# An attention block on one core: queries and keys projected three slots ahead, norm weights folded into the rotation tables, the rms factor applied by ScalarE

## The chip, the cores and the metric

The kernel runs on 1 core of one Trainium2 chip. The metric is device time in microseconds (us) of that core, lower is better; the median of three runs is given. One further execution was recorded by the profiler.

## The reference, cut to what matters

Four batches of 1024 tokens with 512 features are normalised (layernorm, no weights), go through an attention with 16 heads of 128, and are added to an fp8-rounded product of the same normalised tokens with a 512x512 matrix.

```python
xn = layernorm(x)
q  = apply_rope(rmsnorm((xn @ Wq + bq).heads, qn_w), pos)       # 16 heads of 128
lk = apply_rope(rmsnorm((xn @ Wlk + blk).heads, kn_w), pos)
lv = (xn @ Wlv + blv).heads
# entries: softmax-weighted mean of every 4 tokens; ck, cv their key and value, one for all heads
ck = apply_rope(rmsnorm(entries @ Wk + bk, kn_w), block_ends);  cv = entries @ Wv + bv
sparse = softmax over the 8 largest of (q . ck, causal), times cv
local  = softmax over a band of 128 tokens back of (q . lk), times lv
out = x + ((sparse + local) * 0.5) @ Wo + bo + fp8(xn * s) @ fp8(W2 * s1) / (s * s1)
# rmsnorm(x, w) = x * rsqrt(mean(x*x) + eps) * w
# rope on the first 64 of 128: x1*cos - x2*sin, x1*sin + x2*cos; the rest unchanged
```

## The kernel before, in words

The tokens are cut into 32 chunks of 128: chunk `t` is chunk `c = t % 8` of its batch. The 16 heads are taken two at a time, which gives 8 units for a chunk, `u = 0..7`, and 256 units in all, n = 8t + u. Everything is written out by hand in one loop over slots (L789): slot s works on several units at once, at different stages, and each engine takes its instructions in the order in which the loop body issues them. In slot s, with t and u of s:

- `scores` (L561): TensorE makes the scores of unit s for both heads in two PSUM banks (`sc`), against the keys of the chunk before (L570), its own (L577) and the compressed entries (L580, 32(c+1) columns).
- `weigh` and `settle` (L590, L621): VectorE masks the window, finds the 8 largest (L603 to L609), ScalarE takes the exponentials (L610, L618), VectorE keeps and scales the chosen ones (L625 to L636), and ScalarE scales the window (L641).
- `queries` (L438): TensorE projects queries and keys of unit s+2 into one bank `qp` (L443), with a bias product (L444). `squares` (L450): ScalarE squares and sums (L294), and `spread` has GpSimd make the factor r = (mean + eps)^-0.5 (L288, L289).
- `turn` (L652) transposes the probabilities of unit s in 32x32 blocks on VectorE, and sends them through DRAM so that they come back turned (`fetch`, L696, SyncE's queue).
- `values_of` (L530): TensorE projects the values of unit s+1 into `vp`; `keep_values` (L544) has ScalarE copy them out. `values` (L706) multiplies the probabilities of unit s-1 with the values into `cp`, `keep_context` (L727) copies that to `cT` on ScalarE, and `to_output` (L744) multiplies unit s-2 with Wo.
- `normalize` (L459) makes rotated and normed queries and keys of unit s+2: four VectorE operations (L465) multiply `qp` by r and the norm weight into `th`; `rotate` (L296) has GpSimd make th*sin into `rb` (L307), VectorE th*cos (L308), a difference and a sum (L309, L310). `turn_keys` and `fetch_keys` (L504, L524) transpose blocks on VectorE (L510, L513), write them to DRAM with four DMAs (L518), and read them back as `qT` and `lkT` (L528). The first eight units and the last instead go through TensorE (`turn_keys_here`, L482, `keep_keys`, L490).

Two generators run beside it, one step at each of the two calls of `steps()` in a slot (L809, L815). `chunk_prep(t+2)` starts in slot u=7 of chunk t and takes nine slots: layernorm statistics on VectorE (L327, L328), the normalised and transposed tokens `xnT`, the entries, and in its last slot (u=7 of chunk t+1) a transpose on TensorE into a bank `cp` of the pool `pp` (L410) that VectorE copies to `ckT` (L412). One slot earlier (u=6) it norms and rotates the entry's key: VectorE L402, then GpSimd `rb_e` (L307). `chunk_eight(t)` starts in slot u=3 of chunk t: three VectorE operations (L261 to L265) and four GpSimd operations (L266, L268, L270, L272) round the tokens to fp8 over two slots; two slots after the start TensorE multiplies them (`fp`, L423), VectorE reads that (L428), and GpSimd adds it to `x_sum` (L429).

PSUM has eight banks: two `qp`, two `sc`, one `ctx`, one `out`, and two of the pool `pp`, which are taken in turn by everything else: `xp`, `yp`, `ep`, the `cp` of `chunk_prep`, `fp`, and every unit's `vp`. A tile of `pp` waits until what stood two tiles before in that order has been read.

The lines of the loop that set the order around the change:

```python
for_unit(s, (weigh, 0), (weigh, 1))
for_unit(s + 2, (queries,))
for_unit(s, (settle, 0), (settle, 1))
steps()
for_unit(s + 2, (squares, (0, 1, 2, 3)), (spread,))
for_unit(s, (settle_window, 0), (settle_window, 1))
for_unit(s - 2, (to_output,))
steps()
turn(s)
for_unit(s + 1, (values_of,))
for_unit(s + 2, (normalize,))
```

Of the kernel before, what the change touches and what calls it, by code (L numbers as in the profile page):

```python
# [12 lines left out]
F32 = mybir.dt.float32  # L13
# [3 lines left out]
ALU = mybir.AluOpType  # L17
AX = mybir.AxisListType

P = 128  # L20
D = 128
RATIO = 4
ROPE = 64
HALF = ROPE // 2
BLK = 32
NB = P // BLK
# [12 lines left out]
def kernel(  # L39
# [26 lines left out]
    nc = tc.nc  # L66
# [4 lines left out]
    NU = NH // 2  # L71
    NE = P // RATIO
    NT = B * NCH
    NN = NT * NU
# [3 lines left out]
    work = ctx.enter_context(tc.tile_pool(name="work", bufs=2))  # L78
# [5 lines left out]
        return v.rearrange("p (b i) -> p b i", i=BLK)  # L84

    def scratch(name, shape=(P, 512), dtype=F32):
        return work.tile(list(shape), dtype, tag="scratch", name=name, bufs=3)

    def pp(name):
        return psum.tile([P, 512], F32, tag="pp", name=name, bufs=2)  # L90
# [5 lines left out]
    x_tiles, angles = {}, {}  # L96

    def load_x(t, purpose):

        b, c = divmod(t, NCH)  # L100
        xt = work.tile([P, HID], F32, tag="x", name=f"x_{purpose}_{t}")
        nc.sync.dma_start(xt, hidden[b, ts(c, P), :])
        x_tiles[purpose, t] = xt
# [15 lines left out]
    wo_sb = [const.tile([P, 2, HID], F32, name=f"wo_{u}") for u in range(NU)]  # L119

    def load_wqk(u, engine):
        for i, w in enumerate((Wq, Wlk)):
            engine.dma_start(
                wqk_sb[u][:, :, ts(i, 256)], w[:, ts(u, 256)].rearrange("(k p) n -> p k n", p=P)
            )
# [34 lines left out]
    norm_w = const.tile([P, 2, D], F32, name="norm_w")  # L160
# [6 lines left out]
    scales = const.tile([P, 2], F32, name="scales")  # L167
# [84 lines left out]
        nc.tensor.transpose(bp[:, 0:NH], blv_n, ident[:NH, :NH])  # L252
        nc.scalar.activation(blvT, bp[:, 0:NH], AF.Copy, scale=0.5)

    def quantize(dst, src, scalar, tag):

        v = scratch(f"qv_{tag}") if tag[0] == "x" else src
        m = scratch(f"qm_{tag}")  # L260
        nc.vector.tensor_scalar(v, src, scalar, None, ALU.mult)  # L261
        nc.vector.tensor_scalar(
            m.bitcast(U32), v.bitcast(U32), 0x7F800000, None, ALU.bitwise_and
        )
        nc.vector.tensor_scalar(m, m, FP8_MIN_NORMAL, 1.5 * 2.0**20, ALU.max, ALU.mult)  # L265
        nc.gpsimd.tensor_tensor(v, v, m, ALU.add)  # L266
        yield
        nc.gpsimd.tensor_tensor(v, v, m, ALU.subtract)  # L268
        yield
        nc.gpsimd.tensor_scalar(m, v, FP8_OVERFLOW, 0.0, ALU.mult, ALU.mult)  # L270
        yield
        nc.gpsimd.tensor_tensor(dst, v, m, ALU.add)  # L272
        yield

    w2_sb = const.tile([P, KK, HID], BF16, name="w2_sb")


    w2_raw = [wo_sb[NU // 2 + k][:, 0, :] for k in range(KK)]

    def round_w2():  # L280
        for k in range(KK):
            yield from quantize(w2_sb[:, k, :], w2_raw[k], scales[:, 1:2], f"w2_{k}")

    def rstd_of(ss, n, mul, eps, name):

# [10 lines left out]
    def rotate(th, cs, nh, a, name):  # L296

        p = th.shape[0]
        a = a.rearrange("p (h t f) -> p h t f", h=nh, t=2)
        bb = work.tile([P, 4, 2, HALF], F32, tag="ropeb", name=f"rb_{name}", bufs=1)  # L300
        bb = bb[:p, 0:nh]
        x12 = th[:, :, 0:ROPE].rearrange("p h (t f) -> p h t f", t=2)

        def wide(v):
            return v.unsqueeze(1).unsqueeze(1).to_broadcast([p, nh, 2, HALF])

        nc.gpsimd.tensor_tensor(bb, x12, wide(cs[:, HALF:ROPE]), ALU.mult)  # L307
        nc.vector.tensor_tensor(a, x12, wide(cs[:, 0:HALF]), ALU.mult)  # L308
        nc.vector.tensor_tensor(x12[:, :, 0, :], a[:, :, 0, :], bb[:, :, 1, :], ALU.subtract)  # L309
        nc.vector.tensor_tensor(x12[:, :, 1, :], a[:, :, 1, :], bb[:, :, 0, :], ALU.add)  # L310
# [104 lines left out]
    def chunk_eight(t):  # L415

        xt, xnT = x_tiles["sum", t], chunks[t]
        x8 = work.tile([P, KK * P], BF16, tag="x8", name=f"x8_{t}", bufs=1)
        src = xnT.rearrange("p k s -> p (k s)")
        yield from quantize(x8, src, scales[:, 0:1], f"x_{t}")  # L420
        fp = pp(f"fp_{t}")
        for k in range(KK):
            nc.tensor.matmul(  # L423
                fp, x8[:, ts(k, P)], w2_sb[:, k, :], start=(k == 0), stop=(k == KK - 1)
            )
        yield
        f = scratch(f"f_{t}")
        nc.vector.scalar_tensor_tensor(f, fp, inv, bo_sb, ALU.mult, ALU.add)  # L428
        nc.gpsimd.tensor_tensor(xt, xt, f, ALU.add)  # L429
# [4 lines left out]
    def place(n):  # L434

        return divmod(n, NU)
# [18 lines left out]
    def spread(n):  # L455
        w = units[n]
        w["r"] = rstd_of(w["ss"], 4, 1.0 / D, EPS_RMS, f"r_{n}")

    def normalize(n):  # L459
        t, u = place(n)  # L460
        w = units[n]
        qp, r = w.pop("qp"), w["r"]
        th = work.tile([P, 4, D], F32, tag="th", name=f"th_{n}", bufs=1)
        for i in range(4):
            nc.vector.scalar_tensor_tensor(  # L465
                th[:, i, :],
                qp[:, ts(i, D)],
                r[:, i : i + 1],
                norm_w[:, i // 2, :],
                ALU.mult,  # L470
                ALU.mult,
            )
        thb = work.tile([P, NB, 2, 2 * BLK], F32, tag="thb", name=f"thb_{n}", bufs=1)
        spare = thb.rearrange("p b t x -> p (b t x)")[:, 0 : 4 * ROPE]
        rotate(th, angles[t][0], 4, spare, f"{n}")
        w["th"], w["thb"] = th, thb

    def by_dma(n):

        return NU <= n < NN - 1  # L480
# [15 lines left out]

    def key_tiles(n):
        w = units[n]
        qT = work.tile([P, NB, 2 * BLK], F32, tag="qT", name=f"qT_{n}")
        lkT = work.tile([P, NB, 2 * BLK], F32, tag="lkT", name=f"lkT_{n}", bufs=NU + 2)  # L500
        w["qT"], w["lkT"] = qT.rearrange("p a (i g) -> p (a i) g", g=2), lkT
        return qT, lkT

# [267 lines left out]
    def until(g, step):  # L771
        for at in g:
            if at == step:
                break

    def for_unit(n, *todo):
        if 0 <= n < NN:
            for f, *more in todo:
                f(n, *more)

    first, rounding = chunk_prep(0), round_w2()
# [4 lines left out]
    pick_tokens()  # L786
    masks()

    for s in range(-2, NN + 2):  # L789
        t, u = place(s)  # L790

        if s == -2 or u == 7 and 0 <= t and t + 2 < NT:
            running = [*running[-2:], chunk_prep(t + 2)]
        if u == 3 and 0 <= t < NT:
            load_x(t, "sum")
            running = [*running[-2:], chunk_eight(t)]
        if u == 4 and 0 <= t and t + 2 < NT:
            load_x(t + 2, "norm")

        for_unit(s, (scores, 0), (scores, 1))  # L800
        for_unit(s - 2, (keep_context,))
        for_unit(s, (weigh, 0), (weigh, 1))
        for_unit(s + 2, (queries,))
        if not by_dma(s + 1) and s < NU:
            for_unit(s + 1, (turn_keys_here,))
        for_unit(s, (settle, 0), (settle, 1))
        if s < 0:
            until(first, "B4" if s == -2 else "B6")
        steps()  # L809
        for_unit(s + 2, (squares, (0, 1, 2, 3)), (spread,))  # L810
        if not by_dma(s + 1) and s < NU:
            for_unit(s + 1, (keep_keys,))
        for_unit(s, (settle_window, 0), (settle_window, 1))
        for_unit(s - 2, (to_output,))
        steps()  # L815
        if by_dma(s):
            turn(s)
        if s == -1:
            until(first, "B7")
        for_unit(s + 1, (values_of,))  # L820
        if s == -1:
            until(first, "B8")
        if not by_dma(s):
            for_unit(s, (turn_here,))
        for_unit(s + 2, (normalize,))
        for_unit(s - 1, (values,))
        if by_dma(s):
            fetch(s)
        else:
            for_unit(s, (keep_turned,))  # L830
        if s + 2 >= NU:
            for_unit(s + 2, (turn_keys,), (fetch_keys,))
        for_unit(s + 1, (keep_values,))
        if s < NU:

            if s == -1:
                late_constants()
                for k in range(KK):
                    nc.scalar.dma_start(w2_raw[k], input2[ts(k, P), :])
            if 0 <= s < KK:  # L840
                for _ in range(4):
                    next(rounding, None)
            if 3 <= s + 5 < NU:
                load_wqk(s + 5, nc.scalar)
            if 3 <= s + 4 < NU:
                load_wlv(s + 4, nc.scalar)
            if 0 <= s + 1 < NU:
                load_wo(s + 1, nc.scalar)
        if u == 6 and 0 <= t and t + 2 < NT:
            load_angles(t + 2)  # L850
        units.pop(s - 1 - NU, None)
# [46 lines left out]
```

## Time and profile before

| what | us |
|---|---|
| median of three runs | 2830.24 (2829.55 to 2833.36) |
| the profiled execution, its own time | 2828.88 |
| its span, first to last instruction | 2827.2 |
| TensorE busy | 2775.0 (98%) |
| VectorE busy | 2277.4 (81%) |
| ScalarE busy | 1302.9 (46%) |
| GpSimd busy | 818.0 (29%) |

All times below count from the span's start. In a timeline a row holds the start, the duration, the engine, the line, the operation, out<-in, shapes and how many instructions were merged in the row; in brackets stand the engine's idle time before it and what ended it. A matmul of two fp32 operands is recorded as two instructions. The ends of matmuls are modelled, and overlap the next start, so that the pace of TensorE is read from start to start. A few matmul records are missing, most of L444 among them (58 of 256 are there).

### The profile page before, as it was taken

Reading aid. Unit: us, or ns where it says so; the run is one execution under the profiler, and the core shown is the slowest. Engines: PE = TensorE matmul, PEld = TensorE weight load, DVE = VectorE, ACT = ScalarE, POOL = GpSimd, SP = SyncE. Lnnn points to the kernel's source line nnn. Section 1 sums busy time; section 2 is a strip of 40 time slices with the busy share of each in tenths; the row PEclk is TensorE's granted clock in tenths of the full one; section 3 lists DMA queues with packets and bytes.
Section 4 is the critical chain, followed back from the end, with each engine's and each line's share of the span. In section 5 each row is a group of like instructions: output and inputs, shape, how many; then the busy total and the mean of one; then the engine's idle time right before and its main releaser. Section 6 shows DMA issues by size and latency. Waiting matters only on the chain. (4 is left out here: it accounts for less than half of the span.)

```text
span 2827.2 us, 48528 instructions
## 1 busy us (share of the span) xinstructions
PE 2775.0 (98%) x12770; PEld 1879.6 (66%) x12969; DVE 2277.4 (81%) x9132; ACT 1302.9 (46%) x5075; POOL 818.0 (29%) x1161
## 2 busy tenths in 40 slices
PE   7999999999999999999999999999999999999998
PEld 4666666666666666666666666666666666666666
DVE  5778888888777888888877788888887777888886
ACT  3444444444444444444444444444444444444443
POOL 3433222222233332232223233222223222322222
PEclk9999999999999999999999999999999999999999
DMA  7344445555444445555544444555554444455553
GB/s 224 93 140 133 137 143 151 147 153 146 133 128 133 138 134 149 148 152 151 148 129 123 137 134 138 150 153 147 149 146 124 134 131 131 136 152 151 149 149 116
DMA packets 620851, 399.85 MB, mean 141 GB/s; under 512 B 306880, under 2 KB 573984, under 8 KB 620576
## 3 DMA queue, kind: packets, MB, share of 16 engines
q1 hardware_dynamic: 608352, 383.18, 47.8%
q10 hardware_dynamic: 12224, 13.56, 1.5%
q8 instruction: 105, 1.72, 0.3%
q14 instruction: 170, 1.39, 0.2%
HBM read 212.53 MB, written 184.03 MB: 140 GB/s over the span
## 5 line engine op out<-in xcount | busy, mean ns | idle before, releaser
L443 PE MATMUL qp<-wqk,xnT 128*128 128x512 f32 x2048 | 944.6, 604 | 4.1 <-DMA scales<-in_L_ffn_scale_dram 3.1
L443 PEld LDWEIGHTS qp<-wqk,xnT 128*128 128x128 f32 x2048 | 370.1, 191 | 383.9 <-issue 370.3
L610 ACT ACTIVATE prob<-sc,neg 128x256 f32<-128x256 f32 (+1 forms) x512 | 236.1, 461 | 786.4 <-DVE taken L609 772.5
L535 PEld LDWEIGHTS vp<-wlv,xnT 128*128 128x128 f32 x2048 | 391.1, 191 | 170.4 <-issue 109.5
L535 PE MATMUL vp<-wlv,xnT 128*128 128x256 f32 x2048 | 488.6, 382 | 6.2 <-DVE lkT L495 2.9
L751 PE MATMUL op<-wo,cT 128*128 128x512 f32 x1024 | 488.0, 599 | 6.0 <-ACT cT L733 1.5
L659 DVE STREAM_TRANSPOSE probB<-prob 128x512 f32<-128x512 f32 (+2 forms) x494 | 282.9, 610 | 79.4 <-ACT prob L641 75.8
L294 ACT ACTIVATE junk<-qp 128x128 bf16<-128x128 f32 x1024 | 284.2, 278 | 100.0 <-remote 56.6
L307 POOL TENSOR_TENSOR rb<-th,cs 128x256 f32<-128x256 f32 x256 | 247.4, 966 | 276.5 <-DVE th L465 276.5
L465 DVE SCALAR_TENSOR_TENSOR th<-qp,r,norm_w 128x128 f32<-128x128 f32 x1024 | 282.9, 338 | 45.1 <-POOL r L289 44.9
L751 PEld LDWEIGHTS op<-wo,cT 128*128 128x128 f32 x1024 | 186.5, 190 | 179.2 <-issue 115.9
L547 ACT COPY lv<-vp 128x256 f32<-128x256 f32 x256 | 95.4, 373 | 449.5 <-PE cp L718 393.5
L288 POOL TENSOR_SCALAR r<-ss 128x4 f32<-128x4 f32 x256 | 49.8, 195 | 862.8 <-ACT junk L294 856.4
L718 PE MATMUL cp<-probT,lv 128*128 128x128 f32 x1920 | 298.3, 275 | 0.7 <-DMA probT<-pr 0.7
L718 PEld LDWEIGHTS cp<-probT,lv 128*128 128x128 f32 x1920 | 275.3, 192 | 14.3 <-PE vp L535 1.1
L289 POOL TENSOR_TENSOR r<-r,nhalf 128x4 f32<-128x4 f32 x256 | 259.9, 1015 | 21.4
L718 PE MATMUL cp<-probT,cv 128*128 128x128 f32 x1536 | 255.6, 275 | 0.0
L580 PE MATMUL sc<-ckT,qT 128*128 128x96 f32 (+7 forms) x1024 | 226.2, 303 | 0.0
L641 ACT ACTIVATE prob<-prob,tot 128x256 f32<-128x256 f32 (+1 forms) x512 | 223.0, 484 | 2.1 <-DVE tot L635 2.0
L309 DVE TENSOR_TENSOR th<-thb,rb 128x128 f32<-128x128 f32 x256 | 87.1, 340 | 158.9 <-POOL rb L307 158.9
L577 PE MATMUL sc<-lkT,qT 128*128 128x128 f32 x1024 | 209.7, 287 | 5.4 <-DMA lkT<-qk 3.9
L718 PEld LDWEIGHTS cp<-probT,cv 128*128 128x128 f32 x1536 | 213.2, 192 | 0.0
(123 smaller groups left out, 4003.8 us busy)
## 6 DMA issues: line engine op xcount, KB each, us to landing
pr<-probB SPq DMA_DIRECT2D x127, 512.0 KB, 2.6
probT<-pr SPq DMA_DIRECT2D x508, 128.0 KB, 2.9
qk<-thb SPq DMA_DIRECT2D x992, 64.0 KB, 2.0
pr<-probB SPq DMA_DIRECT2D x96, 384.0 KB, 2.3
probT<-pr SPq DMA_DIRECT2D x384, 96.0 KB, 2.5
qT<-qk SPq DMA_DIRECT2D x248, 128.0 KB, 2.3
lkT<-qk SPq DMA_DIRECT2D x248, 128.0 KB, 2.5
x_norm<-_attn_hidden_states_dram SPq DMA_DIRECT2D x32, 256.0 KB, 3.1
```

The source lines that it names most:

```text
L289: nc.gpsimd.tensor_tensor(r, r, nhalf[: ss.shape[0], 0:n], ALU.pow)
L294: nc.scalar.activation(junk[: src.shape[0]], src, AF.Square, accum_out=acc)
L307: nc.gpsimd.tensor_tensor(bb, x12, wide(cs[:, HALF:ROPE]), ALU.mult)
L443: nc.tensor.matmul(qp, xnT[:, k, :], wqk_sb[u][:, k, :], start=(k == 0), stop=False)
L465: nc.vector.scalar_tensor_tensor(th[:, i, :], qp[:, ts(i, D)], r[:, i : i + 1], norm_w[:, i // 2, :], ALU.mult, ALU.mult,)
L535: nc.tensor.matmul(vp[:, 0:256], xnT[:, k, :], wlv_sb[u][:, k, :], start=(k == 0), stop=(k == KK - 1),)
L580: nc.tensor.matmul(sc[:, spa], q, ckT[:, 0:m], start=True, stop=False)
L610: nc.scalar.activation(prob[:, loc], sc[:, loc], AF.Exp, bias=neg[:, 0:1], scale=-1.0, accum_out=tot[:, 0:1],)
L641: nc.scalar.mul(prob[:, loc], prob[:, loc], tot[:, 0:1])
L659: nc.vector.transpose(pb[:, :, ds(h * g, g), :], prob[:, parts[0] * P : (parts[-1] + 1) * P].rearrange("p (g b i) -> p b g i", b=NB, i=BLK),)
L718: nc.tensor.matmul(blocks(cp[:, h, :]), v, probT[:, :, h * len(parts) + i - parts[0], :], start=(i == parts[0]), stop=(i == parts[-1]),)
L751: nc.tensor.matmul(op, cT[:, h, :], wo_sb[u][:, h, :], start=(u == 0 and h == 0), stop=(u == NU - 1 and h == 1),)
```

## The change

1. Queries and keys are projected, normed and turned three slots ahead (unit s+3) where it was two, and the loop begins at s = -3. `qT` gets three buffers (it had two), `lkT` NU+3. The weights `wqk` are loaded one slot earlier on ScalarE's queue.
2. `make_tables(t)`, new, runs once for each chunk on GpSimd, in slot u=5 of the chunk before: cosine and sine are multiplied by the norm weights of query and key, the rest of `cos` holds the weights themselves.
3. `normalize`: ScalarE multiplies `qp` by r into `thb` (four operations); GpSimd multiplies the halves, crossed, with `sin` (two operations of 128x128); VectorE multiplies all 512 columns by `cos`, and adds the 256 rotated ones.
4. The shared scratch tiles go from three buffers to two, `chunk_eight(t)` starts in slot u=5 where it was u=3, and the rounding of W2 uses an unused part of the `wo` tiles as its scratch.

```diff
     def scratch(name, shape=(P, 512), dtype=F32):
-        return work.tile(list(shape), dtype, tag="scratch", name=name, bufs=3)
+        return work.tile(list(shape), dtype, tag="scratch", name=name, bufs=2)
...
+    def make_tables(t):
+        cs, _ = angles[t]
...
+        nc.gpsimd.tensor_tensor(
+            cos[:, :, 0:ROPE].rearrange("p g (t f) -> p g t f", t=2),
+            halves, wide(cs[:, 0:HALF], 2, 2), ALU.mult)
+        nc.gpsimd.tensor_copy(cos[:, :, ROPE:D], norm_w[:, :, ROPE:D])
+        nc.gpsimd.tensor_tensor(
+            sin[:, :, 1, :], halves[:, :, 0, :], wide(cs[:, HALF:ROPE], 2), ALU.mult)
+        nc.gpsimd.tensor_scalar(cs[:, HALF:ROPE], cs[:, HALF:ROPE], -1.0, None, ALU.mult)
+        nc.gpsimd.tensor_tensor(
+            sin[:, :, 0, :], halves[:, :, 1, :], wide(cs[:, HALF:ROPE], 2), ALU.mult)
...
     def normalize(n):
...
         for i in range(4):
-            nc.vector.scalar_tensor_tensor(
-                th[:, i, :], qp[:, ts(i, D)], r[:, i : i + 1], norm_w[:, i // 2, :],
-                ALU.mult, ALU.mult)
-        rotate(th, angles[t][0], 4, spare, f"{n}")
+            nc.scalar.mul(xr[:, ts(i, D)], qp[:, ts(i, D)], r[:, i : i + 1])
+        for i in range(2):
+            nc.gpsimd.tensor_tensor(
+                rb[:, :, :, i, :], xr[:, :, :, ds((1 - i) * HALF, HALF)],
+                heads_of(sin[:, :, i, :]), ALU.mult)
+        nc.vector.tensor_tensor(all_, xr, heads_of(cos), ALU.mult)
+        nc.vector.tensor_tensor(
+            turned, turned, rb.rearrange("p g h t f -> p (g h) (t f)"), ALU.add)
...
-    for s in range(-2, NN + 2):
+    for s in range(-3, NN + 2):
...
         if u == 3 and 0 <= t < NT:
             load_x(t, "sum")
+        if u == 5 and 0 <= t < NT:
             running = [*running[-2:], chunk_eight(t)]
...
+        if u == 5 and t + 1 < NT:
+            make_tables(t + 1)
...
-        for_unit(s + 2, (queries,))
+        for_unit(s + 3, (queries,))
...
-        for_unit(s + 2, (squares, (0, 1, 2, 3)), (spread,))
+        for_unit(s + 3, (squares, (0, 1, 2, 3)), (spread,))
...
-        for_unit(s + 2, (normalize,))
+        for_unit(s + 3, (normalize,))
...
-        if s + 2 >= NU:
-            for_unit(s + 2, (turn_keys,), (fetch_keys,))
+        if s + 3 >= NU:
+            for_unit(s + 3, (turn_keys,), (fetch_keys,))
...
-            if 3 <= s + 5 < NU:
-                load_wqk(s + 5, nc.scalar)
+            if 3 <= s + 6 < NU:
+                load_wqk(s + 6, nc.scalar)
```

Line numbers below L458 differ between the two kernels: in the changed one `normalize` stands around L490 to L520, the GpSimd product is L508, the entry's copy to `ckT` L414, and the values' product L579.

More of the change, by code (lines that the diff above doesn't have):

```diff
@@ L253, in late_constants, with quantize @@
         nc.scalar.activation(blvT, bp[:, 0:NH], AF.Copy, scale=0.5)
-    def quantize(dst, src, scalar, tag):
+    def quantize(dst, src, scalar, tag, m=None):
         v = scratch(f"qv_{tag}") if tag[0] == "x" else src
-        m = scratch(f"qm_{tag}")
+        if m is None:
+            m = scratch(f"qm_{tag}")
         nc.vector.tensor_scalar(v, src, scalar, None, ALU.mult)
@@ L281, in round_w2 @@
         for k in range(KK):
-            yield from quantize(w2_sb[:, k, :], w2_raw[k], scales[:, 1:2], f"w2_{k}")
+            spare = wo_sb[NU // 2 + k][:, 1, :]
+            yield from quantize(w2_sb[:, k, :], w2_raw[k], scales[:, 1:2], f"w2_{k}", spare)
     def rstd_of(ss, n, mul, eps, name):
@@ L457, in spread, with wide @@
         w["r"] = rstd_of(w["ss"], 4, 1.0 / D, EPS_RMS, f"r_{n}")
+    tables = {}
+    def make_tables(t):
+        cs, _ = angles[t]
+        cos = work.tile([P, 2, D], F32, tag="cos", name=f"cos_{t}", bufs=1)
+        sin = work.tile([P, 2, 2, HALF], F32, tag="sin", name=f"sin_{t}", bufs=1)
+        halves = norm_w[:, :, 0:ROPE].rearrange("p g (t f) -> p g t f", t=2)
+        def wide(v, *ones):
+            for _ in ones:
+                v = v.unsqueeze(1)
+            return v.to_broadcast([P, *ones, HALF])
+        nc.gpsimd.tensor_tensor(
+            cos[:, :, 0:ROPE].rearrange("p g (t f) -> p g t f", t=2),
+            halves,
+            wide(cs[:, 0:HALF], 2, 2),
+            ALU.mult,
+        )
+        nc.gpsimd.tensor_copy(cos[:, :, ROPE:D], norm_w[:, :, ROPE:D])
+        nc.gpsimd.tensor_tensor(
+            sin[:, :, 1, :], halves[:, :, 0, :], wide(cs[:, HALF:ROPE], 2), ALU.mult
+        )
+        nc.gpsimd.tensor_scalar(cs[:, HALF:ROPE], cs[:, HALF:ROPE], -1.0, None, ALU.mult)
+        nc.gpsimd.tensor_tensor(
+            sin[:, :, 0, :], halves[:, :, 1, :], wide(cs[:, HALF:ROPE], 2), ALU.mult
+        )
+        tables[t] = cos, sin
     def normalize(n):
@@ L462, in normalize, with heads_of @@
         qp, r = w.pop("qp"), w["r"]
+        cos, sin = tables[t]
         th = work.tile([P, 4, D], F32, tag="th", name=f"th_{n}", bufs=1)
+        thb = work.tile([P, NB, 2, 2 * BLK], F32, tag="thb", name=f"thb_{n}", bufs=1)
+        xr = thb.rearrange("p b t x -> p (b t x)")
         for i in range(4):
-            nc.vector.scalar_tensor_tensor(
[L466 to L470, printed above, removed]
+            nc.scalar.mul(xr[:, ts(i, D)], qp[:, ts(i, D)], r[:, i : i + 1])
+        xr = xr.rearrange("p (g h d) -> p g h d", g=2, h=2)
+        rb = work.tile([P, 2, 2, 2, HALF], F32, tag="ropeb", name=f"rb_{n}", bufs=1)
+        def heads_of(v):
+            return v.unsqueeze(2).to_broadcast([P, 2, 2, v.shape[-1]])
+        for i in range(2):
+            nc.gpsimd.tensor_tensor(
+                rb[:, :, :, i, :],
+                xr[:, :, :, ds((1 - i) * HALF, HALF)],
+                heads_of(sin[:, :, i, :]),
                 ALU.mult,
             )
-        thb = work.tile([P, NB, 2, 2 * BLK], F32, tag="thb", name=f"thb_{n}", bufs=1)
-        spare = thb.rearrange("p b t x -> p (b t x)")[:, 0 : 4 * ROPE]
-        rotate(th, angles[t][0], 4, spare, f"{n}")
+        all_ = th.rearrange("p (g h) d -> p g h d", g=2)
+        nc.vector.tensor_tensor(all_, xr, heads_of(cos), ALU.mult)
+        turned = th[:, :, 0:ROPE]
+        nc.vector.tensor_tensor(
+            turned, turned, rb.rearrange("p g h t f -> p (g h) (t f)"), ALU.add
+        )
         w["th"], w["thb"] = th, thb
@@ L498, in key_tiles @@
         w = units[n]
-        qT = work.tile([P, NB, 2 * BLK], F32, tag="qT", name=f"qT_{n}")
-        lkT = work.tile([P, NB, 2 * BLK], F32, tag="lkT", name=f"lkT_{n}", bufs=NU + 2)
+        qT = work.tile([P, NB, 2 * BLK], F32, tag="qT", name=f"qT_{n}", bufs=3)
+        lkT = work.tile([P, NB, 2 * BLK], F32, tag="lkT", name=f"lkT_{n}", bufs=NU + 3)
         w["qT"], w["lkT"] = qT.rearrange("p a (i g) -> p (a i) g", g=2), lkT
@@ L802 @@
         for_unit(s, (weigh, 0), (weigh, 1))
-        for_unit(s + 2, (queries,))
-        if not by_dma(s + 1) and s < NU:
-            for_unit(s + 1, (turn_keys_here,))
+        for_unit(s + 3, (queries,))
+        if s + 2 < NU:
+            for_unit(s + 2, (turn_keys_here,))
         for_unit(s, (settle, 0), (settle, 1))
         if s < 0:
-            until(first, "B4" if s == -2 else "B6")
+            until(first, ("B3", "B4", "B6")[s + 3])
         steps()
-        for_unit(s + 2, (squares, (0, 1, 2, 3)), (spread,))
-        if not by_dma(s + 1) and s < NU:
-            for_unit(s + 1, (keep_keys,))
+        for_unit(s + 3, (squares, (0, 1, 2, 3)), (spread,))
+        if s + 2 < NU:
+            for_unit(s + 2, (keep_keys,))
         for_unit(s, (settle_window, 0), (settle_window, 1))
```

## The prediction

> **What bounds the kernel now.** I read the busy shares first, then TensorE's timeline from start to start, then what ended its gaps, then the queues of GpSimd and VectorE in the slots where the change puts work.
>
> ```profile
> span 2827.2 us, 48528 instructions
> ...
> PE 2775.0 (98%) x12770; PEld 1879.6 (66%) x12969; DVE 2277.4 (81%) x9132; ACT 1302.9 (46%) x5075; POOL 818.0 (29%) x1161
> ```
>
> TensorE's 98% could hide gaps, since matmul ends are modelled. Start to start it is as full as it looks: a projection (L443, eight records) takes 3.44 us, 0.43 each, and in most slots the length is the same to 0.01 us in all four batches (10.01 in chunk 2, u=3; 10.81 in chunk 6, u=6). Such slots have no slack to win, whatever VectorE, ScalarE or GpSimd do in them. What can be won are the slots that are longer than their like. In the timeline of TensorE near 1480 us:
>
> ```profile
> 1478.64 0.39 PE L718 MATMUL cp<-probT,cv 128*128 128x128 f32 x2
> 1480.24 0.47 PE L577 MATMUL sc<-lkT,qT 128*128 128x128 f32 x2 [1.21 <-DMA lkT<-qk]
> ```
>
> From one start to the next 1.60 us pass where 0.22 are usual: the scores wait for keys on their way through DRAM. Adding this excess over all such places (contexts to scores 5.1 and 5.0, first to second score product 3.2) gives 13.4 us in 30 places. That is all that an earlier projection can win in the steady part. The page's waits of TensorE for qT and lkT show less, as they count from modelled ends.
>
> The other waits are at the start. In chunk 0:
>
> ```profile
> 73.09 1.98 PE L751 MATMUL op<-wo,cT 128*128 128x512 f32 x4
> 77.47 3.66 PE L535 MATMUL vp<-wlv,xnT 128*128 128x256 f32 x8 [2.40 <-DVE total L384]
> ```
>
> The values' product waits 2.56 us for a `pp` bank, and its eight matmuls then take 0.43 each instead of 0.215, so another 1.7 us.
>
> **What the Trainium skill says.** "PSUM — Partial Sum Buffer", Engine vs sequencer instructions: ScalarE, VectorE and GpSimd queues are strict FIFO, and matmuls start in program order. The trace agrees; VectorE's rows never leave the loop's order. "Perfetto Trace Analysis", Optimization Strategy: a gap that repeats on the engine that should be saturated can mean too few PSUM buffers; the gap at 75 us is one. "SBUF — State Buffer", SBUF: two separate sides: a VectorE operation with two SBUF inputs and a GpSimd operation exclude each other for a whole instruction. The trace agrees: L309 takes 0.29 us, and 0.69 beside GpSimd's L270 (below). "TensorE: Matmul & The Clock Gate", What's actually happening: an idle window of about 3.4 us halves the clock. Here waits of 2.26 and 2.56 us did it, 1.57 didn't.
>
> **The change part by part.**
>
> *One slot more for keys.* All 13.4 us go: the keys get a slot of about 10 us more. SyncE's queue keeps its order (pr, four probT, four qk, qT, lkT), only for a later unit. What is late next, the turned probabilities, lands some 5 us ahead of need (written 1507.73, fetched from 1509.90, used at 1517.47). **-13.4.**
>
> *Norm and rotation.* VectorE loses 282.9 + 108.8 + 87.1 + 72.5 = 551 us and gains, per unit, a product of 512 columns (0.71 by L308's 425 ns for 256 and 212 ns for 64) and a sum (0.43): 292 us. ScalarE gains 4 x 0.27 to 0.36 us per unit (L733's pairs start 0.27 apart), 280 to 370 us, and stays under 60%. Waiting for r, its products hold back the value copy (L547) and `cT` behind them, which land about 1.3 us later; the projection and the other context products cover that, as `cT` is used 5 us into the slot. GpSimd loses 247 and gains 256 x 0.62 plus 32 tables of about 1.6. None sets the slot, so 0 by itself. But the chain from r to the turned keys matters below: before, th 1.12, rb 0.97 beside L308, L309 and L310 0.5. `rb` took 0.97 for 256 elements where 512 take 1.28 alone, so about 0.6 of it is its own and the rest the wait for L308. After: VectorE's 0.71 and GpSimd's 0.6 exclude each other, so 1.4 from the last ScalarE product to the sum. Bounds: 1.0 if they overlap, 1.4 if not; I take 1.4.
>
> *Rounding moved from u=3 to u=5.* Its two rounding slots are now u=5 and 6, and `fp` (0.86 us of TensorE) comes in u=7. There `chunk_prep`'s `cp` also takes a `pp` bank, so the order becomes cp, fp, vp: with two banks, vp waits for VectorE's copy L412 **in the same slot**. Before, in u=7, the order was vp of the slot before, cp, vp, and L412 gated nothing. Is the copy in time? In chunk 30 (slot start 2717.42):
>
> ```profile
> 2719.07 0.40 DVE L603 CUSTOM_DVE_ANT_0 sc<-sc,mask_b 128x256 f32<-128x256 f32 x1
> ...
> 2724.04 0.19 DVE L412 COPY ckT<-cp 128x32 f32<-128x32 f32 x1
> ```
>
> VectorE began the slot's scores 1.65 us in and copied at 6.62; vp starts at 7.68, and 8.54 with fp ahead. The margin is 1.9 us, less 0.9 because the layernorm statistics (L327, L328) stand before the copy (not in chunk 30). So vp stalls if VectorE begins over about 2.5 us into the slot. The rounding makes it begin late. Slot u=3 of chunk 30 (start 2671.95), GpSimd, then VectorE:
>
> ```profile
> 2679.85 1.27 POOL L266 TENSOR_TENSOR qv_x<-qv_x,qm_x 128x512 f32<-128x512 f32 x1 [7.77 <-DVE row L376]
> 2681.20 0.19 POOL L288 TENSOR_SCALAR r<-ss 128x4 f32<-128x4 f32 x1
> 2681.47 1.02 POOL L289 TENSOR_TENSOR r<-r,nhalf 128x4 f32<-128x4 f32 x1
> 2682.47 1.28 POOL L268 TENSOR_TENSOR qv_x<-qv_x,qm_x 128x512 f32<-128x512 f32 x1
> 2683.74 0.97 POOL L307 TENSOR_TENSOR rb<-th,cs 128x256 f32<-128x256 f32 x1
> 2684.68 0.62 POOL L270 TENSOR_SCALAR qm_x<-qv_x 128x512 f32<-128x512 f32 x1
> ```
>
> ```profile
> 2684.74 0.69 DVE L309 TENSOR_TENSOR th<-thb,rb 128x128 f32<-128x128 f32 x1 [0.62 <-POOL rb L307]
> ...
> 2686.36 0.40 DVE L603 CUSTOM_DVE_ANT_0 sc<-sc,mask_b 128x256 f32<-128x256 f32 x1
> ```
>
> r waits for one addition, rb for another, and VectorE begins slot u=4 3.60 us late. After the change u=5 does this to u=6, so u=6 begins 3.6 late (the 0.4 of L309 gained, the 0.4 of the chain lost). In u=6 GpSimd's order is rb_e, L270, r, L272, rb, and rb_e waits for VectorE's L402, which follows `settle`. With 5.05 us from L603 to the end of L636: 3.6 + 5.05, L402 0.38, rb_e 0.35, L270 0.68, r 1.29, L272 1.31, products 1.42, sum 0.48, turning 0.73: 15.3, less the slot's 10.81 is 4.5 us late in u=7. There: 4.5 + 5.05 + statistics and copy 1.15 = 10.7 against 8.54: **a stall of 2.1 us.** The same with each chunk's own start in u=4, its scores and slot lengths gives, for c = 0 to 7, 1.1, 1.1, 1.5, 2.0, 1.5, 1.8, 2.1, 2.5 (0.2 off for c under 4, where the slot before leaves more time): 13.6 per batch. Four batches, less the last chunk (no `cp`, 2.5) and chunk 30 (no statistics, 0.9): 51. Bounds: 0.4 less in each of the two chains takes 0.8 from 31 stalls, 26; half a microsecond more per stall, 67. **+51.**
>
> *Start and end.* The rounding left u=3 of chunk 0, where its 1.4 us (75.61 to 77.01) stand ahead of the copy that vp waits for: up to 1.4 + 1.7 won. The third slot ahead puts a projection (3.7) where TensorE waits for th (23.7 to 27.3) and before the first scores, which is work only moved. I take -3, bounds -6 and +3. At the end a third slot has no projection to cover the probabilities' way: +1, bounds 0 and +4. The tables wait for the last product of the chunk before and are done early in u=5: 0; a microsecond late would cost nothing, as r comes 6 us into the slot. One scratch buffer less: each new tile follows its predecessor's last reader by a slot: 0.
>
> *Sum.* -13.4 + 51 - 3 + 1 = +36. On the profiled execution's own 2828.9 (2827.2 of span and 1.7 around it) that is 2865; the median stands 1.4 above it, so **2866**.
>
> **Rivals.**
> - *Faster: the copy is in time.* If u=7 begins within 2.5 us, only the gains stand: 2830 - 13.4 - 3 + 1 = 2815. For it: slots u=7 begin 1.3 to 2.2 late now. Against it: u=4, the model of u=6, begins 3.1 to 3.9 late, and u=6 adds rb_e's wait.
> - *No change.* Stalls of 0.5 us each just pay for the keys: 2830. It needs u=7 to begin 1.2 us earlier than I find.
> - *The clock falls too.* Stalls of 2 us and more (11 of them) halve the clock for a window, 1.7 each: 2885; if all 31 do, over 2910. For it: 2.26 and 2.56 did. Against it: most stalls are shorter.
> - *The change doesn't do what it says*, because keys wait for something else: the bracket above names their DMA, so I give this nothing of its own.
>
> **How the numbers follow.** The stall 0.58, the faster case 0.20, no change 0.08, the clock 0.14. Faster or slower by 0.2% (5.7 us) is about what a measurement can tell from no change: slower 0.72, same 0.08, faster 0.20. The likeliest case alone spans 2840 to 2882 by its bounds. The range, 2814 to 2888, takes in most of the faster case and of the clock, and leaves under 0.2 out.
>
> **What would show it.** No TensorE wait for qT or lkT in the steady part; in u=7 of 31 chunks vp waits for VectorE's copy of `ckT`, 1 to 2.5 us, growing with c; VectorE begins u=6 about 3.6 and u=7 about 4.5 us late; other slots keep their lengths. Wrong if u=7 begins under 2.5 us late, or if vp there follows the output product directly.

## The result, and the profile after

The changed kernel takes 2871.88 us (median of four runs, 2868.98 to 2874.73), the kernel before 2829.89 beside it: ratio 1.0153, interval 1.0141 to 1.0166. It is slower, by 42 us where 36 were forecast. The profiled execution has a span of 2867.8 us, against 2827.2.

The head of the page after, and four of its groups (busy time, mean ns of one, then the idle time of the engine ahead of them and what ended most of it):

```profile
span 2867.8 us, 49183 instructions
...
PE 2773.8 (97%) x12771; PEld 1875.9 (65%) x12969; DVE 2041.4 (71%) x7852; ACT 1562.6 (54%) x6099; POOL 983.0 (34%) x1577
...
L579 PE MATMUL vp<-wlv,xnT 128*128 128x256 f32 x2048 | 491.1, 383 | 49.4 <-DVE ckT L414 43.6
...
L500 ACT ACTIVATE thb<-qp,r 128x128 f32<-128x128 f32 x1024 | 292.7, 368 | 252.5 <-POOL r L291 244.2
L508 POOL TENSOR_TENSOR rb<-thb,sin 128x128 f32<-128x128 f32 x512 | 350.2, 704 | 230.5 <-ACT thb L500 228.2
L515 DVE TENSOR_TENSOR th<-thb,cos 128x512 f32<-128x512 f32 x256 | 186.1, 727 | 321.9 <-ACT thb L500 321.0
```

VectorE lost 236 us of work, and the span grew by 41 all the same. TensorE's work is the same; the values' product (L579, before L535) now waits 43.6 us for VectorE's copy of `ckT` (L414, before L412). The list of TensorE's waits has it with the total in us, the number of places and the longest:

```profile
PE vp L579 <- DVE ckT L414: 43.6, 30, 2.6
```

In the kernel before, in slot u=7 of chunk 27 (c = 3), the values' product follows the output product without a wait:

```profile
2453.81 1.98 PE L751 MATMUL op<-wo,cT 128*128 128x512 f32 x4
2455.64 1.89 PE L535 MATMUL vp<-wlv,xnT 128*128 128x256 f32 x8
```

The same slot after, which starts at 2484.30, in the timeline of TensorE and then of VectorE:

```profile
2489.68 0.24 PE L412 MATMUL cp<-ident,kv 32*128 32x32 f32 x1
2489.86 1.04 PE L425 MATMUL fp<-w_sb,x 128*128 128x512 bf16 x4
2490.73 1.88 PE L795 MATMUL op<-wo,cT 128*128 128x512 f32 x4
2494.43 1.99 PE L579 MATMUL vp<-wlv,xnT 128*128 128x256 f32 x8 [1.82 <-DVE ckT L414]
```

```profile
2489.07 0.40 DVE L647 CUSTOM_DVE_ANT_0 sc<-sc,mask_b 128x256 f32<-128x256 f32 x1
...
2493.40 0.69 DVE L329 BATCH_NORM_STATS2 lnst<-x_norm 128x6 f32<-128x512 f32 x1
2494.12 0.18 DVE L330 BATCH_NORM_AGGREGATE lnst<-lnst 128x2 f32<-128x6 f32 x1
2494.22 0.16 DVE L414 COPY ckT<-cp 128x32 f32<-128x32 f32 x1
```

VectorE begins the slot's scores 4.77 us late, and ends the copy at 2494.38. TensorE, which has made `cp`, `fp` and the output product by then, starts vp 0.05 us later, 3.70 us after the first of four output records that take 0.43 each: a stall of 1.98. From start to start 30 slots u=7 stall by 0.94 to 2.75 us, 48.4 in all.

The time by part of the span, from start to start of TensorE ("middle" is from the first score product of unit 8 to that of unit 248):

| part | before | after | difference |
|---|---|---|---|
| up to unit 8, less the one projection more (3.66) | 123.2 | 123.7 | +0.5 |
| middle | 2605.4 | 2642.6 | +37.1 |
| from unit 248, with the projection less added | 98.6 | 101.5 | +3.0 |

In the middle, the slots u=5 together became 29.9 us shorter and the slots u=7 76.6 longer: 25.8 of both is `fp`, which moved (0.86 in 30 chunks). The waits of scores for their keys, 13.4 us in 30 places before (11.8 of it in the middle, the rest one wait in the last chunk), are down to 0.4.

### The profile page after: what moved, and what is told of

It is laid out like the page before. It is cut to its first block, busy times and chain, and to the rows that moved or that the text cites. A ratio compares the mean times of both kernels' runs of the same rounds, so it can differ in the third digit from the quotient of the medians.

```text
span 2867.8 us, 49183 instructions
## 1 busy us (share of the span) xinstructions
PE 2773.8 (97%) x12771; PEld 1875.9 (65%) x12969; DVE 2041.4 (71%) x7852; ACT 1562.6 (54%) x6099; POOL 983.0 (34%) x1577
## 5 line engine op out<-in xcount | busy, mean ns | idle before, releaser
L579 PE MATMUL vp<-wlv,xnT 128*128 128x256 f32 x2048 | 491.1, 383 | 49.4 <-DVE ckT L414 43.6
L579 PEld LDWEIGHTS vp<-wlv,xnT 128*128 128x128 f32 x2048 | 388.6, 191 | 222.9 <-issue 96.9
L500 ACT ACTIVATE thb<-qp,r 128x128 f32<-128x128 f32 x1024 | 292.7, 368 | 252.5 <-POOL r L291 244.2
L508 POOL TENSOR_TENSOR rb<-thb,sin 128x128 f32<-128x128 f32 x512 | 350.2, 704 | 230.5 <-ACT thb L500 228.2
L515 DVE TENSOR_TENSOR th<-thb,cos 128x512 f32<-128x512 f32 x256 | 186.1, 727 | 321.9 <-ACT thb L500 321.0
L517 DVE TENSOR_TENSOR th<-th,rb 128x256 f32<-128x256 f32 x256 | 116.6, 455 | 182.7 <-POOL rb L508 182.7
L647 DVE CUSTOM_DVE_ANT_0 sc<-sc,mask_b 128x256 f32<-128x256 f32 (+1 forms) x512 | 202.6, 396 | 8.2 <-PE sc L625 7.7
```

The source lines that it names most:

```text
L500: nc.scalar.mul(xr[:, ts(i, D)], qp[:, ts(i, D)], r[:, i : i + 1])
L508: nc.gpsimd.tensor_tensor(rb[:, :, :, i, :], xr[:, :, :, ds((1 - i) * HALF, HALF)], heads_of(sin[:, :, i, :]), ALU.mult,)
L579: nc.tensor.matmul(vp[:, 0:256], xnT[:, k, :], wlv_sb[u][:, k, :], start=(k == 0), stop=(k == KK - 1),)
```

## The experiments

Theory: the three places of cp, fp and vp in two banks make TensorE wait for VectorE, which is late in u=7. Rivals: the late VectorE costs as much wherever `fp` stands; the new norm and rotation cost, not the moved rounding; or the moved rounding alone makes the stalls. Ratios are to runs of the kernel before on the same chip. "Middle" is from one trace of each kernel; e7 and e9, which are the same kernel, differ by 3.3 us there, so a difference of that size says little. Line numbers in these kernels differ by a few.

| kernel (keys three slots ahead unless said) | norm and rotation | rounding from | fp in | ratio (interval) | middle |
|---|---|---|---|---|---|
| before (keys two ahead) | old | u=3 | u=5 | 1 | 2605.4 |
| after | new | u=5 | u=7 | 1.0153 (1.0141 to 1.0166) | 2642.6 |
| e1 | new | u=5 | u=0 | 0.9996 (0.9987 to 1.0004) | 2600.3 |
| e2, copy first | new | u=5 | u=7 | 1.0044 (1.0030 to 1.0058) | 2617.0 |
| e3 (keys two ahead) | old | u=5 | u=7 | 1.0028 (1.0019 to 1.0038) | 2616.8 |
| e4 | old | u=3 | u=5 | 0.9957 (0.9945 to 0.9969) | 2590.6 |
| e5 | old | u=5 | u=7 | 1.0024 (1.0014 to 1.0034) | 2606.6 |
| e6 | old | u=5 | u=0 | 0.9962 (0.9950 to 0.9975) | 2590.9 |
| e7 | new | u=3 | u=5 | 1.0009 (1.0001 to 1.0017) | 2598.3 |
| e9, e7 once more | new | u=3 | u=5 | one run | 2601.6 |
| e8 | old, 0.86 longer | u=3 | u=5 | 1.0662 (1.0646 to 1.0677) | 2771.7 |
| e10 | new, by pairs | u=3 | u=5 | 0.9976 (0.9967 to 0.9986) | 2590.5 |
| e11 | new, by pairs | u=5 | u=7 | 1.0170 (1.0156 to 1.0185) | 2649.2 |
| e12 | old, 0.28 longer | u=3 | u=5 | 1.0011 (1.0003 to 1.0019) | 2601.3 |

### e1: the rounded product one slot later

```diff
         yield from quantize(x8, src, scales[:, 0:1], f"x_{t}")
+        yield
+        yield
         fp = pp(f"fp_{t}")
```

> The changed kernel, with the rounded product fp issued one slot later (u=0 of the next chunk), so that it no longer takes a pp bank in the slot of cp. Bank-order theory: vp in u=7 again has the vp of the slot before two places ahead of it, so the 50 us of waits for VectorE's copy of ckT go, and the two half-clock windows (3.4) with them: 2871.9 - 50.3 - 3.4 = about 2818, although VectorE still begins u=7 about 4 us late. Rival (VectorE's lateness, or the new norm and rotation chain itself, costs the time, whatever bank fp has): the stalls only change their place, 2860 or more.

Measured: 2826.65 us. The stalls of vp are gone to the last one, and u=7 is down to 10.65 us in the mean (13.24 after, 10.69 before), though VectorE begins u=7 as late as ever (3.9 to 6.0 us). So the bank order is what turns lateness into lost time. But almost 9 us of the forecast gain are missing. TensorE's waits in this kernel name where a part of them went:

```profile
PE cp L764 <- DMA probT<-pr: 6.5, 6, 3.6
...
PE sc L626 <- DVE ckT L414: 2.3, 5, 0.8
```

The scores of the next chunk need the same `ckT`, and in five chunks its copy now ends too late for them; and late probabilities come back late from DRAM. (The longest wait, 3.6, stands in the last chunk, where the changed kernel has one of 3.7 as well; in the middle the waits for probabilities are 2.8 us in four places.) The lateness, let go in one place, meets the next readers. The middle is 9.7 us above that of e4, and these waits name 5.1 of it.

### e2: the statistics behind the copy

```diff
-        nc.vector.bn_stats(st[:, 0:6], xt)
-        nc.vector.bn_aggr(st[:, 6:8], st[:, 0:6])
-        r = rstd_of(st[:, 7:8], 1, 1.0, EPS_LN, f"lnr_{t}")
         yield "A0"
+        nc.vector.bn_stats(st[:, 0:6], xt)
+        nc.vector.bn_aggr(st[:, 6:8], st[:, 0:6])
+        r = rstd_of(st[:, 7:8], 1, 1.0, EPS_LN, f"lnr_{t}")
```

> The changed kernel, with the layernorm statistics of u=7 (0.69 + about 0.2 us on VectorE) issued half a slot later, so that they stand behind the copy of ckT. Bank-order theory: each of some 29 stalls gets 0.9 us shorter, none vanishes wholly but those of c = 1 and 4: -26, and the two half-clock windows (3.4) may go with the stalls of over 2.3 us: about 2843 to 2846. Rival (vp waits for another thing that comes at about the same time): no change, 2872.

Measured: 2841.5, a little less than forecast. Two VectorE instructions of 0.9 us together, moved past the copy with the small GpSimd step that reads them, give 0.85 us in the mean of the slots u=7 (12.39 against 13.24), 25.4 in all. So VectorE's queue in the slot sets the stall.

### e3 and e5: the moved rounding with the old norm and rotation

```diff
             load_x(t, "sum")
-            running = [*running[-2:], chunk_eight(t)]
+        if u == 5 and 0 <= t < NT:
+            running = [*running[-2:], chunk_eight(t)]
```

> The kernel before, with nothing changed but the start of chunk_eight, u=5 where it was u=3. If the moved rounding alone makes the stalls, with the old norm and rotation and keys two slots ahead, they come here too: 2830 + about 48, less 1.4 at the start: 2876, between 2865 and 2885. Rival (the ScalarE products and the third slot are what costs): 2830.

Measured: 2836.48, +0.28% where +1.6% was expected. The stalls come, but short: VectorE begins u=7 2.6 to 3.5 us late (c from 1 on), not 3.7 to 4.8, and waits of TensorE for `ckT` sum to 9.5 us in 15 places, where after has 43.6 in 30. The rounding alone is not the whole cause. e5 is the changed kernel with `normalize` as before and no tables:

> The changed kernel with norm and rotation as before (VectorE multiplies by r and the weights, then rotates; no tables), so keys three slots ahead, rounding from u=5, fp in the slot of cp. Theory: the stalls need both, the rounding in u=5 and 6 and the longer way from r to the turned keys; without the second VectorE begins u=7 about 1 us earlier, as with the rounding alone (2.6 to 3.5 us), and the stalls sum to 13 to 16 us: keys alone 2816.8 + 13 = 2830. Rival (the third slot ahead is what makes u=7 later than with the rounding alone): 2850 or more.

Measured: 2832.36. VectorE begins u=7 at 2.8 to 3.5 us (c from 1 on), as in e3, so there the third slot adds nothing to the lateness. For c = 0 it does: 2.2 us in e3, 4.1 in e5. What is left is the norm and rotation, with its tables. In the slot u=5 of chunk 27, GpSimd and then VectorE of e5:

```profile
2438.53 1.01 POOL L291 TENSOR_TENSOR r<-r,nhalf 128x4 f32<-128x4 f32 x1
2439.52 1.27 POOL L269 TENSOR_TENSOR qv_x<-qv_x,qm_x 128x512 f32<-128x512 f32 x1
2440.78 0.97 POOL L309 TENSOR_TENSOR rb<-th,cs 128x256 f32<-128x256 f32 x1
```

```profile
2441.79 0.29 DVE L311 TENSOR_TENSOR th<-thb,rb 128x128 f32<-128x128 f32 x1 [0.62 <-POOL rb L309]
...
2443.01 0.40 DVE L635 CUSTOM_DVE_ANT_0 sc<-sc,mask_b 128x256 f32<-128x256 f32 x1
```

and of after, the same slot:

```profile
2473.37 1.04 POOL L291 TENSOR_TENSOR r<-r,nhalf 128x4 f32<-128x4 f32 x1
2474.36 1.29 POOL L269 TENSOR_TENSOR qv_x<-qv_x,qm_x 128x512 f32<-128x512 f32 x1
2475.66 1.32 POOL L508 TENSOR_TENSOR rb<-thb,sin 128x128 f32<-128x128 f32 x2
```

```profile
2475.68 0.98 DVE L515 TENSOR_TENSOR th<-thb,cos 128x512 f32<-128x512 f32 x1 [2.93 <-ACT thb L500]
2477.01 0.42 DVE L517 TENSOR_TENSOR th<-th,rb 128x256 f32<-128x256 f32 x1 [0.35 <-POOL rb L508]
...
2478.17 0.40 DVE L647 CUSTOM_DVE_ANT_0 sc<-sc,mask_b 128x256 f32<-128x256 f32 x1
```

From the end of r to VectorE's next scores it is 3.47 us in e5 and 3.76 in after. In u=6 and 7 the medians are 3.46 and 3.82: there the new way is 0.36 us longer, because `rb` and VectorE's product hold each other up (L515 takes 0.98 us here, 0.69 as a rule) and take 1.3 us together behind the last ScalarE product. In u=0, 3, 4 and 5 it is 0.25 to 0.45 longer; in u=1 and 2, where the old way is longest (4.1 and 5.0), it is 0.2 to 0.3 shorter. In a row of slots whose length only just holds VectorE's round the difference adds up. Chunk c = 3 on average: VectorE begins u=5, 6 and 7 at 1.13, 3.07 and 3.54 us with the old way, at 1.67, 3.93 and 4.77 with the new.

### e4 and e6: without the new norm and rotation

e4 is the kernel before with keys three slots ahead; of the rest of the change it has only the two scratch buffers, for space. e6 is e5 with `fp` one slot later as in e1.

> The kernel before with queries and keys three slots ahead, and nothing else of the change: norm and rotation as before, rounding from u=3. (For space two scratch buffers and a tile of its own for y.) Theory: the 13 us of waits for keys go, the start and the end lose about 3: 2820. If the keys' wait were only replaced by another: 2830. If a longer start counts in full: 2834.

Measured: 2816.78. The middle falls by 14.9 us; no wait for `qT` or `lkT` is left.

> The same, with fp also one slot later (u=0). Theory: the 10 us by which the changed kernel with a later fp (2826.7) stays above the keys alone (2816.8) come from VectorE's lateness, which now meets the next chunk's scores (they need the same ckT) and the turned probabilities; with the old chain the copy is about 1 us earlier and in time: 2817 to 2820. Rival (fp in u=0, or rounding from u=5, costs these 10 us itself): 2826.

Measured: 2815.03, as good as e4. So with the old norm and rotation neither the rounding in u=5 nor `fp` in u=0 costs anything, and e1's missing 9 us belong to the new one (e1 is 9.4 above e6 in the middle). e4 and e6 both beat both kernels; their intervals overlap.

### e7: the new norm and rotation with the old rounding

```diff
-        if u == 5 and 0 <= t < NT:
             running = [*running[-2:], chunk_eight(t)]
...
-        y = scratch(f"y_{t}")[:, 0 : 2 * D + 1]
+        y = xt[:, 0 : 2 * D + 1]
```

> The changed kernel with chunk_eight starting in u=3 as before (for space y lies in the token tile that is no longer needed): keys three slots ahead, ScalarE products and tables. Theory: the new norm and rotation by itself costs nothing, since no wait of TensorE hangs on VectorE in u=4 and 5: 2817, within 4 of the keys alone. Rival (the longer way from r to the keys costs by itself, or VectorE's relief gains): 2827 or more, or 2810 or less.

Measured: 2827.97, a miss. The new norm and rotation costs by itself, 7.7 us of the middle over e4 and 10.9 of the span. VectorE begins the slots of c = 3 and u=0 of c = 4 3.9 to 6.5 us late, where e4 has 1.6 to 3.9; the slots u=1 of c = 4 are longer (11.96 us in the mean against 11.04), behind a wait for late probabilities in one of them and, in three, waits whose end the profile doesn't name. e9 is the same kernel once more, under a name that doesn't fit it:

> The changed kernel with the old rounding start once more, for its trace beside the next one: 2828 on the chip before.

Measured: 2829.93 in its one run, with VectorE late in the same chunks. Its middle is 11.0 us above e4.

### e8 and e12: the old way, made longer

```diff
         nc.gpsimd.tensor_tensor(bb, x12, wide(cs[:, HALF:ROPE]), ALU.mult)
+        if nh == 4:
+            nc.gpsimd.tensor_scalar(bb, bb, 1.0, None, ALU.mult)
```

> The kernel with keys three slots ahead alone (2816.8), plus one needless GpSimd multiplication by 1 of rb (128 x 256, about 0.35 us) in the old norm and rotation of every unit, between rb and the sum that waits for it. Theory: what the new norm and rotation cost beside the old rounding (2828.0 against 2816.8) is the 0.3 us by which they lengthen the way from r to the next scores on VectorE: in chunks c = 1 to 4, whose slots are shortest, VectorE no longer catches up and begins 4 to 6 us late, so that probabilities come late. Then 0.35 us in the old chain does the same: 2826 to 2831. Rival (ScalarE's products, which wait for r ahead of its other work, are the cost): 2817 to 2819.

Measured: 3014.2, far out. The multiplication takes 0.86 us in the mean, not 0.35, and the way from r to the scores 4.4 us. VectorE then begins its slots some 6 to 10 us late, and TensorE waits 95 us for turned probabilities in 103 places. The direction fits, but so large a delay says little about one of 0.36. So e12 puts in a smaller one, whose size was measured beforehand (in `spread`, `r` times 1):

```diff
         w["r"] = rstd_of(w["ss"], 4, 1.0 / D, EPS_RMS, f"r_{n}")
+        nc.gpsimd.tensor_scalar(w["r"], w["r"], 1.0, None, ALU.mult)
```

> Keys three slots ahead alone (2816.8), plus one GpSimd multiplication by 1 of r itself (128 x 4, 0.19 us, 0.28 from start to start), so that the way from the squares to the next scores is 0.3 us longer, with no other engine or tile touched. Length theory: about as much as the new norm and rotation lengthens it (3.82 against 3.46 us from r to the scores, which cost 11 us in all); a little less: 2822 to 2829. Rival (ScalarE's products, not the length, cost those 11 us): 2817 to 2819.

Measured: 2830.62, 1.6 above the range. 0.3 us more on the way, with ScalarE's work untouched, costs the middle 10.7 us over e4 and makes VectorE late in the same chunks as e7 (5.49 in c = 3, u=0; e7 5.46). So length alone is enough, without ScalarE's products.

### e10 and e11: the new way, made shorter

```diff
+        for g in range(2):
             for i in range(2):
                 nc.gpsimd.tensor_tensor(
-                    rb[:, :, :, i, :], xr[:, :, :, ds((1 - i) * HALF, HALF)],
-                    heads_of(sin[:, :, i, :]), ALU.mult)
+                    rb[:, g, :, i, :], xr[:, g, :, ds((1 - i) * HALF, HALF)],
+                    heads_of(sin[:, g, i, :]), ALU.mult)
+        for g in range(2):
+            # product with cos and sum with rb, each for the pair g
...
```

> The changed kernel with the old rounding start, and norm and rotation cut by pairs of heads: the queries' two GpSimd products and VectorE's product and sum start after the second of four ScalarE products, the keys' after the fourth. Same arithmetic, more and shorter instructions. Theory (length of the way from r to the keys): if that saves about 0.3 of 3.8 us, it is as short as the old one and the time goes from 2828 to about 2817. If GpSimd's and VectorE's shared port makes the four short products no faster than two long ones, the way is not shorter: 2828 or more.

Measured: 2819.85. The way from r to the scores is 3.47 us in u=0, 1, 6 and 7, as short as the old one in u=6 and 7, and the middle is 2590.5, that of e4: there the cost of the new norm and rotation is gone, though ScalarE's products and the tables are still in the kernel. By its ratio e10 is 0.2% slower than e4; in the trace it loses 3.3 us at the start and the end.

> The whole change, with norm and rotation cut by pairs as in the run before. Theory: with the way from r to the keys 0.3 us shorter in each slot, u=7 begins about 1 us earlier, and the stalls of vp fall from 50 to 16 to 20 us: 2872 - 32 = about 2838. Rival (the moved rounding and the bank order alone make the stalls, the chain matters little): 2865 or more.

Measured: 2874.98, a miss: the stalls sum to 48.3 us as after, and the clock is halved behind six of them where it was two (last section). GpSimd's timeline of this kernel, slot u=6 of chunk 27:

```profile
2491.20 1.02 POOL L291 TENSOR_TENSOR r<-r,nhalf 128x4 f32<-128x4 f32 x1
2492.19 1.27 POOL L273 TENSOR_TENSOR x<-qv_x,qm_x 128x512 bf16<-128x512 f32 x1
2493.42 1.40 POOL L510 TENSOR_TENSOR rb<-thb,sin 128x64 f32<-128x64 f32 x4
```

In these slots a GpSimd step of 1.27 us stands between r and `rb` (in u=5 and 6 the rounding, in u=7 the addition to `x_sum`). The first pair is ready early, but GpSimd isn't, and the four short products then all come behind it. There the way is 3.87 us, not 3.47. With the old norm and rotation (e5) the same step is hidden behind VectorE's four products. So in u=5 to 7 the cut gives nothing.

## Why the prediction was right

**The mechanism and most of its size held.** The predicted stalls were 51 us in 31 places; measured 48.4 in 30, and two half-clock windows (1.7 each) beside. By chunk they grow with c as forecast where slots are alike: c = 1 to 3 were 1.1, 1.5 and 2.0, and measured 1.05 to 1.1 (once 2.06), 1.5 and 2.0; c = 4 to 7 were half a microsecond too high (measured 1.0, 1.3 to 1.6, 1.6 to 1.7, 1.9 to 2.2), as u=6 and u=7 begin 3.4 and 4.1 us late for c = 6, not 3.6 and 4.5. The term that was most mis-sized is c = 0: 1.1 forecast, 2.4 to 2.75 measured in three chunks (u=7 begins 5.5 to 5.9 us late), and none in the first. About 1 us of it comes with the third slot: these chunks stall by 0.96 in e5 and not at all in e3. That the sum was so near is in part luck: c = 0 gave 7.6 us for a forecast of 4.4, c = 4 to 7 gave 21.5 for 28.2. The gap at 75 us, which the prediction puts down to too few PSUM buffers, comes once in the kernel before; the one that repeats is this stall.

**The keys.** -13.4 forecast, of which 11.8 lie in the middle; e4 shows -14.9 there, and the 3 us more were not taken apart. The two slots that the prediction gives as the same in all four batches are so in three (10.11 and 11.42 us in the fourth; the second holds a wait for keys, which the 13.4 counts).

**Start and end.** -3 forecast, +0.5 measured; +1 forecast, +3.0 measured. At the start the rounding's absence did shorten one slot (12.6 us where it was 15.0). Set side by side, the traces show the moved rounding winning 1.6 to 2.2 us there (e3 over before, e5 over e4, after over e7), the new norm and rotation losing 1.8 to 2.2 (after over e5, e7 over e4), which the prediction left out, and the third slot losing 0.4 (e4 over before). At the end 1.7 of the 3.0 come with the third slot (e4); the rest wasn't taken apart.

The sum of the middle is then +52.0 (after over e4) - 14.9 = +37.1, and with +0.5 and +3.0 the +40.6 of the span.

**The step that failed** is a sentence on the norm and rotation: "None sets the slot, so 0 by itself." e7 against e4 shows 7.7 us in the middle, although VectorE has a tenth less to do in e7 than before (2066 us against 2277); e10, with the way cut short, shows it gone. It is not VectorE's work that counts in the shortest slots but its round: scores, exponentials, squares, r, products, sum, turning, next scores, each waiting for the one before on another engine. The prediction had priced the longer way at 0.4 (measured 0.25 to 0.45 where it is longer), but used it for the stalls alone. GpSimd's busy time, which by its sums would have fallen by about 40 us, rose by 165: `rb` takes 1.41 us a unit, not 0.62. From the last ScalarE product to the sum it is still 1.4 us (2475.58 to 2477.01 in chunk 27, u=5), as forecast.

**Two causes, not one.** The prediction put the stalls down to "The rounding makes it begin late", with the longer chain as a correction of 0.4 in each of two slots. In the middle of the traces, over e4: the moved rounding alone gives 16.0 us (e5), the new chain alone 7.7 (e7; 11.0 in e9), both 52.0. About half needs both. The lower bound of the stalls (26, with the chain 0.4 shorter in each of the two) stands for the rounding with the old chain, whose stalls are 14.0 in e5. What the two slots leave out is that u=5 already begins later: for c = 3 the new way is behind e5 by 0.54 us in u=5, 0.86 in u=6 and 1.23 in u=7. The total came out right since both causes lay in the changed kernel.

**The rivals.** That the copy is in time failed, as did no change. The clock: 11 stalls of 2 us and more were to halve it; there were six, and two did, of 2.38 and 2.75 us, while 2.47 and 2.21 did not (last section). "The change doesn't do what it says": the keys' waits are gone, so it does.

## What to carry to other kernels

When a step moves, list who shares its pool of PSUM banks in its new slot: a tile two places back whose reader is late in the same slot becomes a wait of TensorE, though nothing in the step itself reads it. An engine at 71% can still be late: in a software pipeline its round through the other engines has to fit the shortest slot, and taking work off it by a detour over two engines may lengthen that round. Lateness that is let through at one place (e1) is met again by the next reader, so take it away at its source (e10 with the old rounding, e6), and look at what stands ahead of the shortened step on its own queue (e11).

## What the runs showed of the hardware

- The clock doesn't follow the length of one wait alone. After: halved for 3.4 us from 829.9 and 2236.1, behind stalls of 2.38 and 2.75 us, not behind 2.47. In e11 vp's matmuls slow down behind six stalls, the shortest of 2.07 us, and not behind one of 2.24. "TensorE: Matmul & The Clock Gate", What's actually happening, in the Trainium skill speaks of an idle window of about 3.4 us; the waits that halved the clock here were shorter.
- What goes with it is where the wait lies. In each trace the halved stretches start on one grid of 3.413 us (829.9 and 2236.1 are 412 steps apart), and what counts is how long TensorE is idle inside one step. In chunks 8 and 24 of after it idles 2.22 and 2.59 us, 2.20 and 2.24 of it in the step before the halved one. In chunk 16 it idles 2.31, but a step ends at 1533.00 and parts this into 1.86 and 0.45: the clock stays full. In e2 a wait of 2.75, parted into 1.86 and 0.89, does nothing; in e3 one of 1.96 within a step does. From unit 8 to 248 of all fourteen traces ten steps have 1.9 us or more of idle time, and each is followed by a halved one; under that, one of 1.80 (e8) is, and none of the others up to 1.86. This is read from the traces; no run moved a wait against the grid.
- GpSimd's multiplication of 128 x 256 by a number took 0.86 us in e8, each time and while VectorE was idle; the one of 128 x 512 by two numbers in the rounding takes 0.61 (L271 of after). So width alone doesn't set this time; what does was not tried.
- Cut by pairs (e10), GpSimd's products take 0.385 us in the mean for 128 x 64 (0.31 to 0.62) where 128 x 128 took 0.70 (0.45 to 0.97): 1.54 us a unit against 1.41. The cut wins by an earlier start, not by less work.
